# Layer 3's gate silu(x Wz) of a four-layer network: computed in the final stage from x3, where it was computed within layer 1, stored and loaded

## The chip, the cores and the metric

The kernel runs on one core of one Trainium2 chip. The metric is device time in microseconds (us) of one execution. Engines are named as in the profile: PE is TensorE's matmul, PEld its weight load, DVE is VectorE, ACT is ScalarE, POOL is GpSimd, SP is SyncE, which only issues transfers here.

## What is computed

Four layers run one after the other over 4 images of 64 x 64 positions and 128 channels, in float32: a neighbourhood attention (layer 0), a full attention over the 4096 positions of an image (layer 1), a gated mixing with a layer norm (layer 2) and a selective scan in four directions (layer 3). The change concerns layer 3, whose input x is called x3 in the kernel:

```
xz = x @ Win
xb, z = jnp.split(xz, 2, axis=-1)
...                                   # xb: convolution, silu, scans in four directions
y = (y0 + y1 + y2 + y3).transpose(0, 2, 1)
zf = jax.nn.silu(z.reshape(Bb, L, Cd))
yz = y * zf
mu = yz.mean(-1, keepdims=True)
xc = yz - mu
var = (xc * xc).mean(-1, keepdims=True)
yn = gamma * xc / jnp.sqrt(var + 1e-05) + beta
out = yn @ Wout
```

`Win` has 128 rows and 512 columns: 256 for xb and 256 for z, the gate.

## The kernel before

**Tiles and stages.** An image of 4096 positions is cut in 8 chunks of 512 (`CH`). A tile has 128 channels on the partitions and 512 positions beside them; the 256 inner channels of layer 3 are two such tiles, f = 0 and 1. `layers_0_to_2` runs the images one after the other, `layer_3` then all of them together.

**Within an image** layer 1 (`layer_1`) loops over 32 blocks of 128 queries plus two turns. In each turn it computes the scores of one block (L624), the softmax of the one before (maxima turned at L639, spread at L647, subtracted at L650, Exp at L651) and the values of the one before that (L657). At the end of each turn, `between(i)` adds work that has nothing to do with this block: layer 2 of the chunks that are ready (`turn`, `mix`, `add`, `norm`, one after the other for each chunk) and, by `front`, the first part of layer 3. `front` takes chunks of the image before and of this image by a list (`takes`): it loads a chunk of x3 (`load`), projects it to xb (`project`, L799), convolves it over some turns, applies Silu (`activate`), computes the scan's inputs (`lower`) and computes the gate (`gate`, L823 to L832: two products of 128 x 512 at L828, two Silus at L820 and two stores of 256 KB to `zf_d` at L832). In the turns it is called with r == 3, once every four turns. The last chunks of image 3 have no layer 1 beside them; they are written out by turn number in `end`.

**The order.** A scheduler orders each engine's instructions by when they are ready, unless an instruction is tied to the one before it on its engine (`keep_in_program_order`, called `pin`). All PE, DVE, ACT and SP instructions of the final stage are pinned; those on POOL aren't. Transfers issued by SP form one queue in order.

**Layer 3.** The scans (L1207 to L1321) run over pairs of images and directions, and add their outputs in `y_d` and `ys`. The **final stage** is the second block of `layer_3`. It loops over 32 chunks j, with these steps:
- `load` (four chunks ahead): two loads of the scans' sum (`yl`, L1356) and two of the gate (`zc`, L1357), 256 KB each; `load_turned` brings 2 MB an image.
- `add_turned` (two ahead): adds the turned directions on POOL (L1374). For every fourth chunk half of it is copied on ACT (L1371) and added by PE later.
- `times_gate` (one ahead): the product with the gate on DVE (L1379), or for every fourth chunk a sum through PE (L1383) and two products (L1384, L1385).
- `project(j, p)` for each half p: turns (L1398) and projects (L1402) on PE, variances by DVE (L1406, L1407) and by ACT (L1409, L1411).
- `root` (L1419): Sqrt of the variances on ACT; a reciprocal on DVE follows in `give_out` (L1425).
- `give_out` (one behind): scales and adds the bias on DVE (L1429), stores from ACT's queue (L1434).

In a turn j these stand as `load(j+4)`, `project(j, 0)`, `give_out(j-1, 0)`, `add_turned(j+2)`, `times_gate(j+1)`, `project(j, 1)`, `root(j)`, `give_out(j-1, 1)`.

Of the kernel before, what the change touches and what calls it, by code (L numbers as in the profile page):

```python
# [80 lines left out]
@with_exitstack  # L81
def conv_seq(ctx, tc, x, mata, matb, cols, rows, rpb, dtw, convw, sel, out):
    nc = tc.nc
    xf = x.rearrange("b h w c -> b (h w) c")
    of = out.rearrange("b h w c -> b (h w) c")

    dram = ctx.enter_context(tc.tile_pool(name="dram", bufs=1, space=DRAM))
    const = ctx.enter_context(tc.tile_pool(name="const", bufs=1))
    x3_d = [dram.tile([P, L], F32, name=f"x3_d{b}") for b in range(B)]

    def stored(name):
        return [[dram.tile([P, L], F32, name=f"{name}{b}_{f}") for f in range(2)] for b in range(B)]

    ub_d, zf_d = stored("ub_d"), stored("zf_d")
# [11 lines left out]
    fronts = x3_d, ub_d, zf_d, y_d, dbl_d, ct_d, gw_d, bw_d  # L108
# [26 lines left out]
    layer_3(tc, of, dt, na, ident, cl, big, early, *fronts)  # L135


@with_exitstack
def layers_0_to_2(
    ctx, tc, xf, mata, matb, rows, rpb, convw, sel, ident, cl, dram, big, ring, early, x3_d, ub_d, zf_d, y_d, dbl_d, ct_d, gw_d, bw_d  # L140
):
    nc = tc.nc
    wp = ctx.enter_context(tc.tile_pool(name="wa", bufs=1))
# [79 lines left out]
            dma(dst, src)  # L223


    win = wp.tile([P, 2 * DI], F32, name="win")
    nc.sync.dma_start(win, matb[:, MB["win"][0]:MB["win"][1]])
# [467 lines left out]
    def layer_2(b, xt):  # L695
# [47 lines left out]
        def norm(n):  # L743
            mv, rd = kept.pop(n)
            for k in range(4):
                x = xt[:, 4 * n + k, :]
                nc.vector.tensor_scalar(x, x, mv[:, k, 0:1], rd[:, k:k + 1], ALU.subtract, ALU.mult)
            stays = b == B - 1 and n >= 4
            if stays:
                x3 = fresh[n] = tmp.tile([P, CH], F32, name="x3k", tag="g1")  # L750
            else:
                x3 = tmp.tile([P, CH], F32, name="x3", tag="c512", bufs=9)
            transpose_tiles(
                xt, 4 * n, x3,
                lambda o, i: nc.vector.tensor_scalar(
                    in_blocks(o), by_block(i, "r b c"), cl("ln_s"), cl("ln_b"), ALU.mult, ALU.add
                ),
            )
            if not stays:
                nc.sync.dma_start(x3_d[b][:, bass.ts(n, CH)], x3)  # L760

        return turn, mix, add, norm

# [9 lines left out]
    def front(b):  # L773
# [21 lines left out]
        def project(i, n):  # L795
            me = n & 1
            for f in range(2):
                pi = ps_s([P, CH], "pi")
                nc.tensor.matmul(pi, lhsT=win[:, P * f:P * f + P], rhs=x_of[i, n], start=True, stop=True)  # L799
                nc.scalar.copy(xh[:, me, f, 1:RC + 1, :], by_image_rows(pi))  # L800
            row = nc.vector if at_end(i, n) and n > 5 else nc.gpsimd
            if n == 4 and i < b:
                nc.gpsimd.tensor_copy(xh[:, me, :, 0, :], kept_row)
            elif n > 0:
                row.tensor_copy(xh[:, me, :, 0, :], xh[:, 1 - me, :, RC, :])
                row.tensor_copy(xh[:, 1 - me, :, RC + 1, :], xh[:, me, :, 1, :])
# [12 lines left out]
        def silu(i, n, to, of):  # L819
            ins = nc.scalar.activation(to, of, AF.Silu)  # L820
            if not at_end(i, n):
                tc.keep_in_program_order(ins)

        def gate(i, n):
            x = x_of.pop((i, n))
            for f in range(2):
                pz = ps_s([P, CH], "pz")
                nc.tensor.matmul(pz, lhsT=win[:, DI + P * f:DI + P * f + P], rhs=x, start=True, stop=True)  # L828
                zf = tmp.tile([P, CH], F32, name="zf", tag="c512", bufs=9)

                silu(i, n, zf, pz)
                nc.sync.dma_start(zf_d[i][f][:, bass.ts(n, CH)], zf)  # L832

        def tap(n, f, dy, dx):
            r0, r1, c0, c1 = region(n, dy, dx)
# [186 lines left out]
        def end(i):  # L1022

            c = B - 1
            if i in (30, 34, 38):
                n = i // 4 - 2
                load(c, n)
                project(c, n)
            if i == 31:
                gate(c, 5)  # L1030
            if i in (30, 31):
                convolve(c, 4, range(2), i - 30)
            if i == 34:
# [7 lines left out]
                activate(c, 5, True)  # L1041
            if i == 37:
                lower(c, 5)
                gate(c, 6)
            if i == 38:
                convolve(c, 7, (1,), 0)
                convolve(c, 7, (1,), 1)
                for f in range(2):
                    convolve_by_pe(c, 6, f, 1)
                activate(c, 6, True)  # L1050
                convolve_by_pe(c, 7, 0)
                lower(c, 6)
                gate(c, 7)
            if i == 39:
                activate(c, 7, True)
            if i == 40:
# [13 lines left out]
        def turn(i):  # L1070
# [8 lines left out]
            if j < 8:  # L1079
# [7 lines left out]
                elif now and r < 2:  # L1087
                    convolve(*now, range(2), r)
                if r == 3:
                    for c in takes[j]:  # L1090
                        gate(*c)
                    for c in takes[j + 1] if j < 7 else []:
                        load(*c)

# [63 lines left out]


@with_exitstack  # L1160
def layer_3(ctx, tc, of, dt, na, ident, cl, big, early, x3_d, ub_d, zf_d, y_d, dbl_d, ct_d, gw_d, bw_d):
    nc = tc.nc
    def pool(name, bufs=1, **kw):

# [2 lines left out]
    wp = ctx.enter_context(pool("wb"))  # L1167
    gw = wp.tile([P, 2, C], F32, name="gw")
    bw = wp.tile([P, C], F32, name="bw")
    eps = wp.tile([P, 1], F32, name="eps")  # L1170
    ct = wp.tile([W, 2, W], F32, name="ct")

    def place(name, tag, bufs=1):
# [5 lines left out]
    nc.vector.memset(eps, 1e-5)  # L1179
# [38 lines left out]
    with pool("s", 2) as sp, pool("psC", 2, space=PSUM) as psp:  # L1218
# [88 lines left out]
        for j, ((loads, pair), after) in enumerate(zip(todo, todo[1:] + [None])):  # L1307
# [9 lines left out]
            if j == 0:  # L1317
                nc.sync.dma_start(gw, gw_d)
                nc.sync.dma_start(bw, bw_d)
                nc.sync.dma_start(ct[:, 0, :], by_rows(bc_d[B - 1][1])[0])  # L1320
            if j == 18:  # L1321
                turn_c(B - 1, psp.tile([P, 2, CH], F32, name="pt3", tag="dt0", bufs=1)[0:W, 0, 0:W])
# [7 lines left out]
    with pool("o", 2) as op, pool("psD", 2, space=PSUM) as psp:  # L1330
# [18 lines left out]
        def load(j):  # L1349
            b, n = chunks[j]  # L1350
            c = held[j] = Chunk()
            c.yl = op.tile([P, 2, CH], F32, name="yl", tag="yl", bufs=4)
            c.zc = op.tile([P, 2, CH], F32, name="zc", tag="zc", bufs=4)
            lo = L - CH * (n + 1) if b & 1 else CH * n
            for f in range(2):
                pin(nc.sync.dma_start(c.yl[:, f, :], y_d[0][b][f][lo // SC][:, lo % SC:lo % SC + CH]))  # L1356
                pin(nc.sync.dma_start(c.zc[:, f, :], zf_d[b][f][:, bass.ts(n, CH)]))  # L1357

        def add_turned(j):

# [5 lines left out]
            for f, yt in enumerate((yts[b], ys[b])):  # L1366
# [6 lines left out]
                else:  # L1373
                    nc.gpsimd.tensor_tensor(by_rows(c.yc[:, f, :]), by_rows(yn), yr, ALU.add)  # L1374

        def times_gate(j):
            c = held[j]
            if c.sum is None:
                pin(nc.vector.tensor_tensor(c.yc, c.yc, c.zc, ALU.mult))  # L1379
            else:  # L1380
                ps = psp.tile([P, CH], F32, name="ysum", tag="s", bufs=1)
                for i, part in enumerate(c.sum):
                    pin(nc.tensor.matmul(ps, lhsT=ident, rhs=part, start=(i == 0), stop=(i == 1)))  # L1383
                pin(nc.vector.tensor_tensor(c.yc[:, 0, :], ps, c.zc[:, 0, :], ALU.mult))  # L1384
# [2 lines left out]
        def project(j, p):  # L1387
# [3 lines left out]
                c.po = []  # L1391
                c.var = op.tile([P, 4, 2], F32, name="var3", tag="var3", bufs=3)
            py = psp.tile([P, 2, DI], F32, name="py", tag="y", bufs=3)
            po = psp.tile([P, 2, C + 1], F32, name="po3", tag="o", bufs=4)
            for q in range(2):
                ts = bass.ts(2 * p + q, P)
                for f in range(2):
# [18 lines left out]
        def root(j):  # L1416
            c = held[j]
            c.rd = op.tile([P, 4], F32, name="rd3", tag="rd3", bufs=3)
            pin(nc.scalar.activation(c.rd, c.var[:, :, 1], AF.Sqrt, bias=eps))  # L1419

        def give_out(j, p):
            b, n = chunks[j]
            c = held[j]
            if p == 0:
                pin(nc.vector.reciprocal(c.rd, c.rd))  # L1425
                c.ot = op.tile([P, 4, C], F32, name="ot", tag="ot", bufs=3)
            for q in range(2):
                k = 2 * p + q
# [10 lines left out]
        for j in range(-2, last + 1):  # L1439
# [10 lines left out]
                add_turned(j + 2)  # L1450
            if 0 <= j + 1 < last:
                times_gate(j + 1)
            if 0 <= j < last:
                project(j, 1)
                root(j)
# [82 lines left out]
```

## Time and profile before

| | us |
|---|---|
| three runs: median (lowest, highest) | 3702.48 (3697.66, 3703.27) |
| the profiled execution: first to last instruction (span) | 3697.0 |
| layer 1 of image 0 begins (first L639) | 227.5 |
| last product of the layer-1 loops (L657) | 3006.3 |
| scans: first product (L1248) | 3059.4 |
| final stage: first load issued (L1356) | 3527.2 |

The page comes from one execution. The profile gives no time for it but its span, which lies 5.5 us below the median of the runs.

How to read it: a line of the timeline has its start, its time and the number of instructions that run into one another; two products of 128 x 512 in float32 show as four records. A line by stretch has, for each engine, the busy time and the number of instructions, then the granted clock of PE (1.00 is full), the share that the DMA engines were busy, and what they moved. In the 40-slice rows each digit is the busy share of a slice of 92.4 us in tenths.

### The profile page before, as it was taken

How to read it: one execution, taken by the hardware profiler on the slowest of the kernel's cores; microseconds unless marked ns; L12 is line 12 of the kernel's file. 1: busy time of each engine (PE TensorE's matmuls, PEld its weight loads, DVE VectorE, ACT ScalarE, POOL GpSimd, SP SyncE). 2: the span in 40 equal slices, each digit the busy share in tenths (PEclk: the TensorE clock that was granted, in tenths of full speed). 3: DMA queues.
4: the chain of work that ended last, by engine and by line, in shares of the span. 5: the costliest groups of instructions: out<-in, count | busy, mean ns of one | idle time of the engine just before them, and what ended most of it. 6: DMA issues, size and time to landing. Idle time of an engine off the chain costs nothing.

```text
span 3697.0 us, 70138 instructions
## 1 busy us (share of the span) xinstructions
PE 3349.9 (91%) x26774; PEld 2768.1 (75%) x26774; DVE 2796.5 (76%) x5227; ACT 2699.7 (73%) x4387; POOL 1419.4 (38%) x1592
## 2 busy tenths in 40 slices
PE   7999999999999999999999999989999997666647
PEld 4789999966899999667999996779999962222236
DVE  4667788866678878666777886767787767999968
ACT  5856677777677777786777777867777778999934
POOL 6500012244122122451222223512221338999866
PEclk8999999999999999999999999999999995555579
DMA  4200000121010012410121212100100269999998
GB/s 132 64 3 30 13 13 30 60 90 34 18 50 27 33 45 79 134 39 15 42 72 33 76 48 94 45 1 24 47 27 33 70 179 240 217 232 211 209 276 281
DMA packets 188308, 310.95 MB, mean 84 GB/s; under 512 B 22303, under 2 KB 110908, under 8 KB 183068
## 3 DMA queue, kind: packets, MB, share of 16 engines
q1 hardware_dynamic: 145316, 220.27, 17.7%
q0 software_dynamic: 24384, 76.95, 11.7%
q10 hardware_dynamic: 18272, 9.24, 0.9%
q8 instruction: 211, 3.46, 0.4%
q14 instruction: 125, 1.02, 0.1%
HBM read 167.69 MB, written 155.56 MB: 87 GB/s over the span
## 4 chain that ended last, share of the span: by engine, by line
PE 59%; issue 13%; DVE 10%; POOL 8%; ACT 7%; DMA 3%; SPq 1%; DVEq 0%; POOLq 0%; ACTq 0%
PE sc L624 17%; PE po L657 17%; PE pt L502 4%; POOL inp L1259 3%; PE sc L467 3%; PE po L513 2%; POOL y L1301 2%; DVE mx L630 2%; DVE acc L878 1%; PE pp L523 1%; PE pz L828 1%; DVE h L1286 1%; PE pb L647 1%; PE pq L595 1%; PE pk L598 1%
## 5 line engine op out<-in xcount | busy, mean ns | idle before, releaser
L624 PE MATMUL sc<-qT,kT 128*128 128x128 f32 x8192 | 1083.9, 276 | 15.8 <-DVE mx L630 15.8
L657 PE MATMUL po<-v,st 128*128 128x129 f32 x8192 | 1080.6, 275 | 2.0 <-ACT st L651 2.0
L624 PEld LDWEIGHTS sc<-qT,kT 128*128 128x128 f32 x8192 | 1000.9, 193 | 38.8 <-issue 26.6
L657 PEld LDWEIGHTS po<-v,st 128*128 128x128 f32 x8192 | 997.9, 192 | 4.7 <-ACT st L651 2.2
L627 ACT COPY st<-sc 128x512 f32<-128x512 f32 x1024 | 574.8, 584 | 426.2 <-PE sc L624 425.5
L630 DVE TENSOR_TENSOR mx<-mx,sc 128x512 f32<-128x512 f32 x768 | 524.0, 682 | 202.3 <-ACT st L627 178.6
L650 DVE TENSOR_TENSOR st<-st,pb 128x2048 f32<-128x2048 f32 x256 | 574.5, 2280 | 4.9 <-PE pb L647 3.8
L651 ACT ACTIVATE st<-st 128x2048 f32<-128x2048 f32 x256 | 483.2, 1908 | 64.7 <-DVE st L650 64.0
L1248 PE MATMUL pdt<-dbl,dt 8*128 8x512 f32 x512 | 307.3, 1079 | 142.1 <-ACT de L1255 141.1
L1259 POOL TENSOR_TENSOR inp<-de,ub 128x1024 f32<-128x1024 f32 x128 | 409.6, 4393 | 9.0 <-DMA y<-du 4.9
L1248 PEld LDWEIGHTS pdt<-dbl,dt 8*128 8x128 f32 x512 | 114.0, 311 | 332.5 <-ACT de L1255 269.5
L493 POOL TENSOR_SCALAR pr<-pr,sm 128x308 f32<-128x308 f32 (+3 forms) x512 | 243.7, 495 | 219.4 <-DVE sm L491 187.3
L723 POOL TENSOR_TENSOR x<-x,row 128x512 f32<-128x512 f32 x32 | 40.8, 1275 | 692.7 <-PE pt L283 692.7
L869 POOL TENSOR_TENSOR gsum<-gsum,tp 128x504 f32<-128x504 f32 (+1 forms) x177 | 240.7, 1363 | 170.9 <-ACT tp L861 84.1
L485 ACT ACTIVATE pr<-pr,mx 128x308 f32<-128x308 f32 (+3 forms) x512 | 262.6, 517 | 0.0
L1286 DVE TENSOR_TENSOR_SCAN h<-h,end,inp 128x1024 f32<-128x1024 f32 x96 | 221.1, 2346 | 18.3 <-ACT h L1272 8.0
L471 DVE CUSTOM_DVE_ANT_0 pr<-sc,bias_m 128x266 f32<-128x266 f32 (+1 forms) x384 | 152.1, 452 | 103.6 <-PE sc L467 103.6
L502 PE MATMUL pt<-ident,pr 128*88 128x128 f32 (+5 forms) x1472 | 203.8, 275 | 8.1 <-ACT prT L504 7.8
L1301 POOL DMA_DIRECT2D y<-yo x112 | 200.7, 2710 | 10.8 <-DVE yo L1300 7.9
L878 DVE SCALAR_TENSOR_TENSOR acc<-xh,cc,acc 128x512 f32<-128x512 f32 (+3 forms) x250 | 199.3, 818 | 4.6 <-ACT acc L842 3.6
L502 PEld LDWEIGHTS pt<-ident,pr 128*88 128x88 f32 (+5 forms) x1472 | 163.5, 138 | 45.6 <-ACT prT L504 31.6
L504 ACT COPY prT<-pt 110x512 f32<-110x512 f32 (+3 forms) x240 | 139.1, 580 | 65.6 <-PE pt L502 65.6
(234 smaller groups left out, 5170.9 us busy)
## 6 DMA issues: line engine op xcount, KB each, us to landing
y<-yo POOLq DMA_DIRECT2D x112, 512.0 KB, 10.6
y<-y SPq DMA_DIRECT2D x48, 512.0 KB
zf_d<-zf SPq DMA_DIRECT2D x64, 256.0 KB
ub_d<-u SPq DMA_DIRECT2D x64, 256.0 KB
ub<-ub_d SPq DMA_DIRECT2D x16, 1024.0 KB
yl<-y SPq DMA_DIRECT2D x64, 256.0 KB
zc<-zf_d SPq DMA_DIRECT2D x64, 256.0 KB
v_d<-vt SPq DMA_DIRECT2D x32, 256.0 KB
```

The costliest lines, as they stand in the source:

```text
L485: pin(nc.scalar.activation(k.pr[:, h], k.pr[:, h], AF.Exp, bias=k.mx[:, h:h + 1], accum_out=k.sm[:, h:h + 1]))
L502: pin(nc.tensor.transpose(pt[0:n, h, :], k.pr[:, h, at:at + n], ident))
L624: nc.tensor.matmul(ps[:, r, :], lhsT=kT[:, bass.ts(G * g + r, P)], rhs=qT[:, bass.ts(i, P)], start=True, stop=True)
L627: nc.scalar.copy(k.st[:, G * g:G * g + G, :], ps)
L630: nc.vector.tensor_tensor(k.mx, k.st[:, 0:G, :] if g == 1 else k.mx, ps, ALU.max)
L650: nc.vector.tensor_tensor(part, part, pb.unsqueeze(1).to_broadcast([P, 16, P]), ALU.add)
L651: nc.scalar.activation(part, part, AF.Exp)
L657: nc.tensor.matmul(k.po, lhsT=k.st[:, j, :], rhs=v[:, j, :], start=(j == 0), stop=(j == NT - 1))
L1248: nc.tensor.matmul(pdt[j][:, g, :], lhsT=dt[o:o + RANK, P * f:P * f + P], rhs=at(dbl[o:o + RANK, :], k & 2, g0, g0 + CH), start=True, stop ...
L1259: nc.gpsimd.tensor_tensor(by_rows(inp), by_rows(de), at(ub_s[f], b ^ (k & 1), SC * n, SC * n + SC), ALU.mult)
L1286: nc.vector.tensor_tensor_scan(h[:, way], h[:, way], inp[:, way], prev, ALU.mult, ALU.add)
L1301: nc.gpsimd.dma_start(here if f == 1 and k == 3 else there, yo, accum_op=ALU.add)
```

## The change

The gate leaves `front`, and `zf_d` with its stores and loads goes. All chunks of x3 are stored now, those too that stayed on the chip before (chunks 4 to 7 of image 3). The second half of `Win` is loaded as `wz` during the scans. In the final stage a chunk's x3 is loaded (256 KB instead of two loads of 256 KB), and `gates(j + 2)` computes the gate just ahead of `project(j, 1)`. Three more edits come with it: the root is taken on POOL, by an addition of eps and a power of -0.5, in place of ACT's Sqrt and DVE's reciprocal; the PSUM tag "s" gets two buffers, which the gate and the sum share; and the tag "o" of the output sums gets 3 for 4.

```diff
@@ layers_0_to_2: norm, project, gate, turn
-            if not stays:
-                nc.sync.dma_start(x3_d[b][:, bass.ts(n, CH)], x3)
+            nc.sync.dma_start(x3_d[b][:, bass.ts(n, CH)], x3)
...
+            x_of.pop((i, n))
...
-        def gate(i, n):
-            x = x_of.pop((i, n))
-            for f in range(2):
-                pz = ps_s([P, CH], "pz")
-                nc.tensor.matmul(pz, lhsT=win[:, DI + P * f:DI + P * f + P], rhs=x, start=True, stop=True)
-                zf = tmp.tile([P, CH], F32, name="zf", tag="c512", bufs=9)
-
-                silu(i, n, zf, pz)
-                nc.sync.dma_start(zf_d[i][f][:, bass.ts(n, CH)], zf)
...
-                    for c in takes[j]:
-                        gate(*c)
@@ layer_3
-    eps = wp.tile([P, 1], F32, name="eps")
+    wz = wp.tile([P, DI], F32, name="wz")
+    root4 = wp.tile([P, 4], F32, name="root4")
...
+                nc.sync.dma_start(wz, matb[:, MB["win"][0] + DI:MB["win"][1]])
...
-            c.zc = op.tile([P, 2, CH], F32, name="zc", tag="zc", bufs=4)
+            c.xz = op.tile([P, CH], F32, name="xz", tag="xz", bufs=4)
...
-                pin(nc.sync.dma_start(c.zc[:, f, :], zf_d[b][f][:, bass.ts(n, CH)]))
+            pin(nc.sync.dma_start(c.xz, x3_d[b][:, bass.ts(n, CH)]))
...
+        def gates(j):
+            c = held[j]
+            c.zc = op.tile([P, 2, CH], F32, name="zc", tag="zc", bufs=2)
+            for f in range(2):
+                ps = psp.tile([P, CH], F32, name="zs", tag="s", bufs=2)
+                pin(nc.tensor.matmul(ps, lhsT=wz[:, bass.ts(f, P)], rhs=c.xz, start=True, stop=True))
+                pin(nc.scalar.activation(c.zc[:, f, :], ps, AF.Silu))
...
-                ps = psp.tile([P, CH], F32, name="ysum", tag="s", bufs=1)
+                ps = psp.tile([P, CH], F32, name="ysum", tag="s", bufs=2)
...
-            po = psp.tile([P, 2, C + 1], F32, name="po3", tag="o", bufs=4)
+            po = psp.tile([P, 2, C + 1], F32, name="po3", tag="o", bufs=3)
...
-            pin(nc.scalar.activation(c.rd, c.var[:, :, 1], AF.Sqrt, bias=eps))
+            nc.gpsimd.tensor_scalar(c.rd, c.var[:, :, 1], 1e-5, 1.0, ALU.add, ALU.mult)
+            nc.gpsimd.tensor_tensor(c.rd, c.rd, root4, ALU.pow)
...
-                pin(nc.vector.reciprocal(c.rd, c.rd))
...
             if 0 <= j + 1 < last:
                 times_gate(j + 1)
+            if j + 2 < last:
+                gates(j + 2)
             if 0 <= j < last:
                 project(j, 1)
                 root(j)
```

The three calls of `gate` in `end` (chunks 5, 6 and 7 of image 3) go too, and `win` is loaded with 256 columns for 512.

More of the change, by code (lines that the diff above doesn't have):

```diff
@@ L92, in stored @@
         return [[dram.tile([P, L], F32, name=f"{name}{b}_{f}") for f in range(2)] for b in range(B)]
-    ub_d, zf_d = stored("ub_d"), stored("zf_d")
+    ub_d = stored("ub_d")
     dbl_d = [dram.tile([NDBL, L], F32, name=f"dbl_d{b}") for b in range(B)]
@@ L107, in conv_seq @@
     ]
-    fronts = x3_d, ub_d, zf_d, y_d, dbl_d, ct_d, gw_d, bw_d
+    fronts = x3_d, ub_d, y_d, dbl_d, ct_d, gw_d, bw_d
     ident = const.tile([P, P], F32, name="ident")
@@ L134, in conv_seq @@
     layers_0_to_2(tc, xf, mata, matb, rows, rpb, convw, sel, ident, cl, dram, big, ring, early, *fronts)
-    layer_3(tc, of, dt, na, ident, cl, big, early, *fronts)
+    layer_3(tc, of, matb, dt, na, ident, cl, big, early, *fronts)
 @with_exitstack
 def layers_0_to_2(
-    ctx, tc, xf, mata, matb, rows, rpb, convw, sel, ident, cl, dram, big, ring, early, x3_d, ub_d, zf_d, y_d, dbl_d, ct_d, gw_d, bw_d
+    ctx, tc, xf, mata, matb, rows, rpb, convw, sel, ident, cl, dram, big, ring, early, x3_d, ub_d, y_d, dbl_d, ct_d, gw_d, bw_d
 ):
@@ L223, in layers_0_to_2 @@
             dma(dst, src)
-    win = wp.tile([P, 2 * DI], F32, name="win")
-    nc.sync.dma_start(win, matb[:, MB["win"][0]:MB["win"][1]])
+    win = wp.tile([P, DI], F32, name="win")
+    nc.sync.dma_start(win, matb[:, MB["win"][0]:MB["win"][0] + DI])
     wx = wp.tile([P, 2, HD], F32, name="wx")
@@ L1028, in end @@
                 project(c, n)
-            if i == 31:
-                gate(c, 5)
             if i in (30, 31):
@@ L1043, in end @@
                 lower(c, 5)
-                gate(c, 6)
             if i == 38:
@@ L1052, in end @@
                 lower(c, 6)
-                gate(c, 7)
             if i == 39:
@@ L1160, in layer_3 @@
 @with_exitstack
-def layer_3(ctx, tc, of, dt, na, ident, cl, big, early, x3_d, ub_d, zf_d, y_d, dbl_d, ct_d, gw_d, bw_d):
+def layer_3(ctx, tc, of, matb, dt, na, ident, cl, big, early, x3_d, ub_d, y_d, dbl_d, ct_d, gw_d, bw_d):
     nc = tc.nc
@@ L1178, in layer_3 @@
     ys = [place("y0", "kT")] + [place(f"y{b}", "ring", 5) for b in range(1, B)]
-    nc.vector.memset(eps, 1e-5)
+    nc.vector.memset(root4, -0.5)
     bc_d = [[dbl_d[b][RANK:RANK + 1, :], dbl_d[b][RANK + 1:RANK + 2, :], ct_d[b]] for b in range(B)]
```

## The prediction

> **What bounds the kernel now.** I read the page's first two parts first, then single stretches of the timeline, then busy time by stretch. The whole span is 3697.0 us. The three runs shown are 3697.66, 3702.48 and 3703.27, that is 0.7 to 6.3 us above that span, the median 5.5. All sums below are made against the span, and 5.5 is added at the end.
>
> The page says that TensorE (PE) is nearly always busy until the scans:
>
> ```profile
> PE 3349.9 (91%) x26774; PEld 2768.1 (75%) x26774; DVE 2796.5 (76%) x5227; ACT 2699.7 (73%) x4387; POOL 1419.4 (38%) x1592
> PE   7999999999999999999999999989999997666647
> PEclk8999999999999999999999999999999995555579
> ```
>
> A busy PE need not be a limit, so I look at two turns of layer 1's loop in image 0. A turn runs from one transposed maximum (L639) to the next. This is the PE timeline of a turn with layer 2's `mix` (L708, L712, L716) and no gate:
>
> ```profile
> 376.53 0.27 PE L639 MATMUL pt<-ident,mx 128*128 128x128 f32 x1
> ...
> 387.58 0.29 PE L708 MATMUL pr<-rs,ma 128*128 128x8 f32 x2
> 387.72 1.10 PE L712 MATMUL pg<-x2T,ma 128*128 128x512 f32 x2
> 388.67 1.02 PE L716 MATMUL pl<-x2T,w_le 128*128 128x512 f32 x2
> 389.52 1.05 PE L624 MATMUL sc<-qT,kT 128*128 128x128 f32 x8
> ...
> 393.10 0.27 PE L639 MATMUL pt<-ident,mx 128*128 128x128 f32 x1
> ```
>
> And of a turn with `mix` and the gate (L828):
>
> ```profile
> 440.72 0.27 PE L639 MATMUL pt<-ident,mx 128*128 128x128 f32 x1
> ...
> 453.71 1.88 PE L828 MATMUL pz<-xc,win 128*128 128x512 f32 x4
> 455.43 1.05 PE L624 MATMUL sc<-qT,kT 128*128 128x128 f32 x8
> ...
> 459.00 0.27 PE L639 MATMUL pt<-ident,mx 128*128 128x128 f32 x1
> ```
>
> The first turn takes 16.57 us, the second 18.28. The difference, 1.71, is what the gate's four records hold PE (453.71 to 455.43, 1.72). PE works without a gap, so here its work is time.
>
> The final stage is another matter. Busy time by stretch (PE, PEld, DVE, ACT, POOL, granted clock, DMA share, GB/s):
>
> ```profile
> 3637.00:3667.00 30.00, 23.60 (x180) 20.44 (x179) 27.00 (x76) 14.92 (x55) 23.77 (x14) 1.00 1.00 335
> 3547.30:3687.00 139.70, 105.91 (x774) 92.32 (x775) 115.88 (x310) 61.97 (x222) 93.09 (x54) 0.94 0.90 305
> ```
>
> and its chain of waits, one period of four chunks apart:
>
> ```profile
> 3651.31 0.68 DVE yc L1385
> ...
> 3667.63 0.68 DVE yc L1385
> ```
>
> A period is 16.32 us, 4.08 a chunk, with VectorE (DVE) busy 27.0 of 30. From the first gate product (3547.3) to the last (3686.9) are 31 chunks, 126.5 us at that pace, and 139.6 were taken; 13.1 went to late loads (POOL's add waits 8.48 us for `yl` at 3589.9).
>
> **What goes from layer 1.** 30 of 32 chunks have their gate in or at the end of the layer-1 loops (120 records of L828 up to 3006), the last two behind them.
> - 28 chunks inside full turns: 28 x 1.72 = 48.2. Later turns with a gate take 18.6 to 18.7, not 18.28, with the 0.3 to 0.4 around ScalarE (ACT) work; if that goes as well, 21 turns return up to 7 more. Three turns of 20.0 us (image 1's runs from 1120.9 to 1140.9) have PE idle 1.5 for DVE, and PE waits 2.0 in the turn behind; there the gate may be free, 5 less. I take 3 less: 45.
> - Two chunks at 2986.6, in the last turn: 3.4. Their second pair of Silus, with two table loads, sits between the halves of the last Exp (1.28 + 1.08 + 1.28 = 3.64 on ACT from 2997.08); PE waits 2.00 there. 2.0 more.
> - Chunk 6 of image 3: four records on the chain at 3035.8, 1.7.
> - Chunk 7: ACT does two Silus until 3056.3 ahead of the u of the same chunk (L912), whose sum is ready at 3051.8; ACT is free at 3052.8. I count 2.7 of these 3.4.
>
> Sum 54.8, say 55, with 47 to 66 as ends. The 64 stores (L832) leave SP's queue, where they wait 679.6 us in all; DMA is at a share of 0.15 there, so I count nothing. Four added x3 stores take the place of eight gate stores in the tail: nothing. The table loads mostly stay, since the u of another chunk follows the gate in the same turn. The scans (3059 to 3530) lose nothing and only start earlier; the one added load of 128 KB vanishes among their transfers.
>
> **What comes to the final stage.** For each chunk two products of 128x512 (1.72 of PE), two Silus (2 x 0.597 on ACT), two small GpSimd (POOL) operations; a 0.298 Sqrt on ACT and a 0.145 reciprocal on DVE go. Loads fall from four of 256 KB to three: 49.2 MB in the last 172 us become 40.8, which at 335 GB/s is 122 us. That is under any time below, so the 13.1 of late loads go, and the next late thing is PE.
>
> PE's pace per chunk, from its starts at 3656.33, 3656.79, 3657.69: turns 0.46, projection 0.90, both twice: 2.72. With gates 4.44. Every fourth chunk has the sum through PE (3665.10 to 3666.82, 1.72): 6.16. Four chunks 19.5, against 16.32. 29 chunks at 4.87 and the last two, without gates, at 4.08 make 149.4: +9.8 is the floor.
>
> On top stands a loop, because the po buffers fall from 4 to 3. po(j+2,0) now needs the output sums of j's second half, and these follow the root. From the start of po(j,0): 0.90, gates 1.72, turn 0.46, po 0.90, is 3.98; 0.2 to ACT; its bias, Square and accumulator read, 1.0; the root P on POOL, 0.1; then on DVE two sums 0.52, the gate product 1.66, statistics 0.55, two sums 0.52, and 0.1 back. That is 8.6 + P for two chunks. Of P the trace shows no row: a power on POOL isn't in it. Below stand the 0.10 memset of 128x1, above the 4.39 product of 128x1024. Nearest is the tensor_scalar of 128x128 (0.372), so two operations on 4 columns get 0.5. The loop then gives 4.55 a chunk, 6.27 with the sum: 152.6, **+13**.
>
> Behind the root on POOL stand the adds of chunk j+3; ahead, if the order differs. The POOL lines are not pinned, and the trace shows that POOL takes what is ready: L723 runs behind PE's transposes (692.7 us of idle end there) ahead of L719, which the code writes first. An add becomes ready when po(j,1) has read its buffer, 0.9 ahead of the root. With one add of 1.6 ahead the loop is 9.7, 4.85 a chunk: 161.3, **+22**. With both, 5.65: 184, +45. I take +18, between the first two. The start (POOL waits for a `y` accumulate until 3544.3) and the end (the power instead of Sqrt and reciprocal) change by under 1.
>
> ACT has 0.34 + 1.33 + 0.27 + 0.38 (output issue) + 1.2 = 3.5 a chunk, under the pace. Square and Copy run at 3553 without a table load, then behind the Sqrt load as well, so they seem to be at home in several tables; with Silu's the trace doesn't show Square. Bounds: nothing, or two loads of 1.28 a chunk, 6.1 on ACT, +46. I take nothing, as both tables seen had them; the other end lies where the late root below does.
>
> The Trainium skill, "ScalarE: Activation LUTs", section "Table sets: the hidden batching unit", says that cheap functions (it names relu, copy, identity, abs) are in every set, Square not among the names; with a switch at its 2.66 us twice a chunk ACT would need 8.8 and my sum would end near 3770.
>
> The product on DVE takes 1.21 alone and up to 2.53, POOL's add 1.50 to 2.53: they hinder each other, and the rows I use hold that. The skill's "SBUF — State Buffer", section "SBUF: two separate sides", calls the port that they share an exclusive lock: a DVE instruction with two SBUF inputs shuts a reading POOL instruction out for its whole length. By that the small root could wait for a product, some 1.4 in the loop, 20 us in all, and my sum would end near 3685.
>
> **Sum.** -55 + 18 = -37: span 3660, median 3665.
>
> **Rivals.**
> - *Root behind both adds* (0.16): +45, so -10, 3692. For it: POOL's readiness order. Against: the second add starts only after the root is ready.
> - *More comes back* (0.14): 66 in layer 1 and only the floor of 10: -56, 3646. For it: 18.6 against 18.28. Against: DVE is busy 19 to 20 us in the turns behind the gates.
> - *The power is dear* (0.06): one POOL instruction sets the final stage. It decides from P = 3.4, where the loop is 6.0, 6.43 with its share of the sums, and 29 of these eat the 55. At 4.4 it gives 6.93: 209, +70, 3717, slower. Against: only 4 columns.
> - *Little is gained in layer 1* (0.04): DVE or ACT take over as the limit, 25 instead of 55: 3695. Against: gapless PE rows.
> - The forecast, +13 to +22 (0.60).
>
> The range holds the forecast, the better case, the late root and the fourth, with 4 us of turn-to-turn scatter at the lower end: 3642 to 3696; the dear power and the outer parts of the forecast's own bounds stay out. Faster by over 0.2% (7.4 us, about what a measurement here can tell from none): 0.60 + 0.14 + 0.15, and half of the fourth, 0.91. Within: 0.04. Slower: 0.05.
>
> **What would show it.** Turns of the layer-1 loop with `mix` at 16.6 to 17.0; no L828 and Exp halves together at the end. In the final stage PE the busiest, granted clock 1.0, four chunks 19.5 to 22 apart, DMA share about 0.75, no table load but one. Wrong if POOL's root is longer than 1 us, if POOL does adds ahead of it, or if turns stay above 18.

## The result and the profile after

| | kernel before | changed kernel |
|---|---|---|
| median of 4 runs each (lowest, highest), us | 3701.84 (3697.66, 3703.27) | 3755.14 (3749.41, 3756.36) |
| span of the profiled execution | 3697.0 | 3752.2 |

The ratio is 1.0143, with an interval from 1.0128 to 1.0157: the changed kernel takes 1.4% longer. The prediction was 3665, in a range that ended at 3696. The spans divide like this (layer-1 loops: first L639 to the last product of values; tail: from there to the scans' first product; scans: to the final stage's first load; final stage: to the end):

| us | before | after | difference |
|---|---|---|---|
| layer-1 loops | 2779.1 | 2758.8 | -20.3 |
| tail | 52.8 | 58.4 | +5.6 |
| scans | 467.8 | 471.7 | +3.9 |
| final stage | 169.8 | 236.4 | +66.6 |
| within it, first to last gate product (31 chunks) | 139.5 | 204.4 | +64.9 |

What was ahead of the loops is 0.6 shorter; together that is the 55.2 between the spans. Below, "the stage's 31 chunks" is always the last row.

The page's 40 slices of the changed kernel, PE and the granted clock:

```profile
PE   7999999999999999999999999999999976666587
...
PEclk9999999999999999999999999999999965555699
```

The picture is that of before up to the scans. A turn with `mix` (PE, from one L639 to the next, with layer 2's product between) is now

```profile
1252.97 0.33 PE L639 MATMUL pt<-ident,mx 128*128 128x128 f32 x1 [0.91 <-DVE mx L635]
...
1269.35 0.27 PE L639 MATMUL pt<-ident,mx 128*128 128x128 f32 x1
```

16.38 us, and no L828 is left. That turn in the kernel before took 18.57. The saving is there; other turns gave it back, as the first experiment below shows. The final stage by stretch, with the columns of the prediction's view:

```profile
3625.00:3655.00 30.00, 24.57 (x129) 15.89 (x127) 13.81 (x39) 12.64 (x37) 18.52 (x19) 1.00 0.49 158
3535.20:3739.70 204.50, 167.38 (x892) 113.13 (x890) 102.16 (x280) 88.06 (x253) 115.87 (x113) 0.98 0.51 170
```

The clock is full and the DMA share has fallen from 0.90 to 0.51, as forecast. But no engine is full: PE 24.6 of 30, POOL 18.5, DVE 13.8 where it had 27.0. A stage that is slow with no engine full points to a loop of waits. Its longest wait (engine and line, what it waits for, total, times, longest):

```profile
DVE ot L1423 <- POOL rd L1414: 80.3, 29, 3.4
```

POOL's own timeline in one turn shows why (start, time, line, operation, and in brackets the idle time before it and what ended it). With it stand the last of ACT's sums of squares that the root needs, the instruction of DVE that waits, and two second halves of the projection on PE, po(j,1) and po(j+1,1), with po(j+1,0) and the gates of chunk j+3 between them:

```profile
3638.51 1.53 POOL L1360 TENSOR_TENSOR yc<-yl,cb 128x512 f32<-128x512 f32 x1 [2.00 <-PE po L1396]
3640.00 1.53 POOL L1360 TENSOR_TENSOR yc<-yl,y 128x512 f32<-128x512 f32 x1
3641.61 0.19 POOL L1413 TENSOR_SCALAR rd<-var 128x4 f32<-128x4 f32 x1
3641.89 1.02 POOL L1414 TENSOR_TENSOR rd<-rd,root 128x4 f32<-128x4 f32 x1
```

```profile
3639.09 0.19 ACT L1405 ACTIVATION_READ_ACCUMULATOR sq<-py,nm 128x1 f32 x1
```

```profile
3642.94 0.61 DVE L1423 SCALAR_TENSOR_TENSOR ot<-po,rd,bw 128x128 f32<-128x128 f32 x2 [3.04 <-POOL rd L1414]
```

```profile
3637.30 1.13 PE L1396 MATMUL po<-gm,yc 128*128 128x129 f32 x8 [1.53 <-DVE ot L1423]
...
3643.69 1.13 PE L1396 MATMUL po<-gm,yc 128*128 128x129 f32 x8 [0.92 <-DVE ot L1423]
```

When the products of po(j,1) have read their tile (PE 3637.30 to 3638.43), both adds of chunk j+3 may write it, and both run ahead of the root of chunk j. That root has all it needs at 3639.28, ahead of the second add (3640.00), and the add runs first all the same, in every turn that has two; so POOL's order isn't that of readiness; the scheduler had set it. The root takes 0.19 and 1.02, DVE's sums of the first half 0.61, and they release the buffer that the next po(j+1,1) needs; PE starts it at 3643.69. From 3637.30 to 3643.69 is 6.39 us: one chunk. While DVE stands at `ot`, all that is behind it on DVE (the gate product, the statistics, the sums) waits too, and PE behind these.

### The profile page after: what moved, and what is told of

Its sections match the earlier page's. It is cut to its first block, busy times and chain, and to the rows that moved or that the text cites. A ratio compares the mean times of both kernels' runs of the same rounds, so it can differ in the third digit from the quotient of the medians.

```text
span 3752.2 us, 69998 instructions
## 1 busy us (share of the span) xinstructions
PE 3371.9 (90%) x26774; PEld 2775.7 (74%) x26774; DVE 2790.2 (74%) x5195; ACT 2697.0 (72%) x4363; POOL 1437.6 (38%) x1656
## 3 DMA queue, kind: packets, MB, share of 16 engines
q1 hardware_dynamic: 132212, 196.15, 15.7%
## 4 chain that ended last, share of the span: by engine, by line
PE 54%; DVE 13%; ACT 10%; issue 10%; POOL 9%; DMA 3%; SPq 0%; POOLq 0%; ACTq 0%; DVEq 0%
PE sc L624 15%; PE po L657 15%; PE pt L502 4%; POOL inp L1244 3%; DVE mx L630 3%; PE sc L467 2%; PE po L513 2%; POOL y L1286 2%; ACT st L651 2%; DVE acc L868 2%; ACT st L627 2%; DVE st L650 2%; PE pp L523 1%; POOL yc L1360 1%; PE pi L798 1%
## 5 line engine op out<-in xcount | busy, mean ns | idle before, releaser
L624 PE MATMUL sc<-qT,kT 128*128 128x128 f32 x8192 | 1088.3, 277 | 14.8 <-DVE mx L630 14.7
L650 DVE TENSOR_TENSOR st<-st,pb 128x2048 f32<-128x2048 f32 x256 | 574.8, 2280 | 18.9 <-PE pb L647 18.5
L859 POOL TENSOR_TENSOR gsum<-gsum,tp 128x504 f32<-128x504 f32 (+1 forms) x177 | 232.2, 1318 | 139.1 <-ACT gsum L847 70.7
L1271 DVE TENSOR_TENSOR_SCAN h<-h,end,inp 128x1024 f32<-128x1024 f32 x96 | 221.0, 2346 | 20.3 <-ACT h L1257 10.0
L868 DVE SCALAR_TENSOR_TENSOR acc<-xh,cc,acc 128x512 f32<-128x512 f32 (+3 forms) x250 | 226.1, 913 | 6.4 <-ACT acc L832 5.1
L719 POOL TENSOR_TENSOR o<-o,rt 128x512 f32<-128x512 f32 x32 | 34.1, 1067 | 402.7 <-DVE o L718 397.0
```

What stands on the lines that cost most here:

```text
L624: nc.tensor.matmul(ps[:, r, :], lhsT=kT[:, bass.ts(G * g + r, P)], rhs=qT[:, bass.ts(i, P)], start=True, stop=True)
L650: nc.vector.tensor_tensor(part, part, pb.unsqueeze(1).to_broadcast([P, 16, P]), ALU.add)
L868: nc.vector.scalar_tensor_tensor(acc, x, c, acc, ALU.mult, ALU.add)
```

## Layer 1 and the tail: two losses beside the saving

**u's Silu.** Before, `gate` stood at the end of its turn, and `activate`, the Silu of another chunk's u, came just behind. ACT before, one such turn:

```profile
1273.42 1.28 ACT L820 ACT_TABLE_LOAD   x1
1274.71 1.22 ACT L820 ACTIVATE zf<-pz 128x512 f32<-128x512 f32 x2
1275.83 1.05 ACT L820 ACTIVATE u<-acc 128x1024 f32<-128x1024 f32 x1
```

One load served both, right behind layer 2's Sigmoid. After, with the gate's Silus gone, the Silu of the same chunk's u is placed two turns earlier by the scheduler, behind the softmax and away from the Sigmoid, with a load of its own and a reload for Exp behind it:

```profile
1232.08 1.28 ACT L820 ACT_TABLE_LOAD   x1
1233.38 1.06 ACT L820 ACTIVATE u<-acc 128x1024 f32<-128x1024 f32 x1
...
1241.10 1.28 ACT L651 ACT_TABLE_LOAD   x1
```

Four turns in a row, the first of them with `mix`, took 18.62, 18.54, 15.88 and 15.07 before (from 1192.0, with the gate in the first), and 16.76, 18.15, 16.21 and 17.81 after (from 1184.0, with this u at the end of the third and the reload in the fourth): the gate's turn won 1.9, and the turn with the reload lost 2.7.

*e4_silu_first.* In `between`, u's Silu is moved to the head of its turn, ahead of the convolution:

```diff
+            for c, at in zip(whole, u_at):
+                if c and i == at and at < 32:
+                    activate(*c, False)
             now = whole[j] if j < 8 else None
...
-                if c and i == at:
-                    activate(*c, at >= 32)
+                if c and i == at and at >= 32:
+                    activate(*c, True)
```

> The changed kernel with the Silu of the convolved chunk (u) issued at the head of its turn's extra work, right behind the Sigmoid of layer 2, where the gate's Silus carried it before; the final stage is as in the changed kernel. Theory (the u Silu lost its place beside the gate's and pays a table load and a load back to Exp in a turn of its own, where PE waits 1 to 2.6 us): layer 1's loops, first transposed maximum to last value product, take 2725 to 2742 us where the changed kernel has 2758.8 and the one before 2779.1. Rival (with the gate gone DVE or ACT set the pace of the turns): 2752 to 2762.

Measured (one run): 3719.49. Loops 2725.8, 33.0 less than after and 53.3 less than before; table loads up to the end of the loops 158, against 177 and 169; the four turns 16.92, 18.55, 15.07, 15.10. The final stage is unchanged (204.5). So the gate's removal was worth about what the prediction counted in the loops (50.4 of its 55), and 33.0 of it was lost to the place of u's Silu.

**The ring of tiles.** In the tail, ACT of the changed kernel stands still here:

```profile
3014.35 1.33 ACT L950 ACTIVATE du<-u,col 128x512 f32<-128x512 f32 x2 [8.68 <-DMA y<-du]
```

`du` takes its tile from the tag `c512`, a ring of 9. With the gate's two `zf` gone, fewer tiles pass between two `du`, and the tile whose turn it is was one whose accumulating store (issued by POOL at 3001.82) hadn't landed. SP had started copies of 512 KB from 2998.88 on; that the store stood behind them is argued from these times, not shown.

*c11_more_buffers.* As e4_silu_first, with `bufs=11` for 9 wherever the tag `c512` stands.

> u's Silu at the head of its turn, and 11 buffers for the tag c512 in place of 9; the whole computation. Theory for the tail (with the gate's two tiles gone from this ring, the ninth tile back of a du is a du whose store stands behind copies of the scans' sums, and ACT waits 8.7 us for it): the stretch from the last layer-1 product to the scans' first product falls from 58.2 to 50-54 us, the layer-1 loops stay at 2724-2730, the whole 3711-3716. Rival (the copies and stores are late whatever the ring): 57-59, the whole 3717-3722.

Measured (one run): 3707.85; the wait is gone (`du` starts at 2969.17 right behind the Silu), the tail is 51.1 for 58.2, loops 2722.6. The theory holds for the tail; loops and whole came out a little below what was expected. With both edits loops and tail are 58.2 us below those of before; the prediction had 54.8.

## The final stage: which part costs, and through what

*e5_root_alone.* The kernel before with the root part alone; the gate stays in layer 1:

```diff
-            po = psp.tile([P, 2, C + 1], F32, name="po3", tag="o", bufs=4)
+            po = psp.tile([P, 2, C + 1], F32, name="po3", tag="o", bufs=3)
...
-            pin(nc.scalar.activation(c.rd, c.var[:, :, 1], AF.Sqrt, bias=eps))
+            nc.gpsimd.tensor_scalar(c.rd, c.var[:, :, 1], 1e-5, 1.0, ALU.add, ALU.mult)
+            nc.gpsimd.tensor_tensor(c.rd, c.rd, root4, ALU.pow)
...
-                pin(nc.vector.reciprocal(c.rd, c.rd))
```

with 2 buffers for `ysum`.

> The kernel before with one part of the change: root on POOL by addition and power, 3 buffers for the output sums, 2 for the sum through PE; the gate stays in layer 1 and is loaded. Theory (loop of one turn through POOL): the gate's products aren't in the loop, so the final stage is nearly as slow as with the whole change, 185 to 204 us from the first to the last gate product where the kernel before has 139.5, span 3740 to 3760. Rival (the products and Silus of the gate slow the final stage): 139 to 155.

Measured (one run): 3750.18; the stage's 31 chunks 184.7, 45 more than before.

*e7_no_gate_product.* The other way round: the changed kernel with `pin(nc.scalar.copy(c.zc[:, f, :], c.xz))` for product and Silu, which leaves the gate out.

> The changed kernel without the two gate products on PE and their Silus in the final stage: two ACT copies of the loaded x3 stand in zc instead, and the root stays on POOL. This leaves the gate out, so only its time counts. Theory (the root is most of the loss, the gates about 20 us): the stage from the first to the last gate product falls from 204.4 to 178-190 us, as where the root alone was moved (184.7). Rival (the gates are the price): 140-155.

Measured (one run): 3731.54; 184.9. The two agree: the root is 45 of the 65, the gate's work 20. As ACT copies for as long as it took for a Silu (0.62 and 0.60 us), these 20 are the price of the products on PE and of the waits that they bring.

*e6_no_power.* `ALU.mult` for `ALU.pow`, which leaves the power out.

> The changed kernel with the power on POOL replaced by a multiplication with the same constant, in the same place; this leaves the power out, so only its time counts. A multiplication of 4 columns should take about what the addition takes, 0.2 us, for 1.02. Theory (the root's whole length stands in the loop that DVE closes): about 0.8 us a chunk less over 31 chunks, so from the first to the last gate product 177-187 us for 204.4, the whole 3728-3738. Rival (only its place behind two adds counts, POOL would wait for data in any case): 197-205, the whole above 3745.

Measured (one run): 3729.63; 183.3, 21.1 less. The group of the multiplication (mean in ns behind the comma):

```profile
L1414 POOL TENSOR_TENSOR rd<-rd,root 128x4 f32<-128x4 f32 x26 | 5.2, 201 | 2.2
```

0.82 us shorter per chunk gave 0.68 per chunk: the power's length stands in the loop nearly whole, so the loop closes in each chunk. A loop of two chunks would have given 0.41.

*e1_root_first.* The adds and the root's two instructions are pinned on POOL in the order of the code, so that the root comes ahead of the adds of chunk j+3.

> The changed kernel, with the POOL instructions of the final stage tied to the order of the code, so that the root of chunk j runs ahead of the two adds of chunk j+3 and not behind them. Theory (a loop of one turn): the second projection of a turn needs the output-sum buffer that the first output sums of the chunk before give back; these wait for the root, and the root stands behind two adds of 1.52 us, which wait for the projection before. Without the adds in it the loop is about 4.0 us and PE sets the pace, so the 31 chunks from the first to the last gate product take 152 to 162 us where they took 204.4, and the span is near 3705. Rival (the power's own 1.21 us, or the gate's products on PE with their waits, set the pace): 190 to 204, span above 3738.

Measured (one run): 3722.69; 177.8, 26.6 less, between the theory's range and the rival's. Of the rest, DVE still waits 31.4 us for the root in 29 waits, and two groups have become longer:

```profile
L1360 POOL TENSOR_TENSOR yc<-yl,y 128x512 f32<-128x512 f32 x29 | 58.5, 2019 | 0.0
...
L1373 DVE TENSOR_TENSOR yc<-yc,zc 128x1024 f32<-128x1024 f32 x22 | 44.3, 2012 | 0.0
```

In the changed kernel these means were 1.52 and 1.21: there DVE waited while POOL worked. Now they meet, as here:

```profile
3621.34 1.54 POOL L1360 TENSOR_TENSOR yc<-yl,cb 128x512 f32<-128x512 f32 x1
3622.83 2.50 POOL L1360 TENSOR_TENSOR yc<-yl,y 128x512 f32<-128x512 f32 x1
```

```profile
3621.92 2.03 DVE L1373 TENSOR_TENSOR yc<-yc,zc 128x1024 f32<-128x1024 f32 x1
```

The add that was running keeps its 1.54; the product that starts beside it takes 2.03, and the next add 2.50. How much of the 177.8 comes from this, no run isolates.

*e2_po4.* `bufs=4` for `po3` and, to make room, `bufs=2` for `py`.

> The changed kernel with 4 buffers for the output sums again, and 2 for the turned tiles, where it has 3 and 3; POOL's order as it is, root behind the adds. Theory (the loop is closed by the third buffer): with four, a projection waits for output sums of half a turn earlier, the loop spans more than one turn, and the 31 chunks take 160 to 175 us for 204.4. Rival (the root's lateness alone is enough, whatever the buffers, or the gate's products are the price): 195 or more.

Measured (one run): 3751.38; 200.0. My theory named the third buffer as what closes the loop, and that failed: one more buffer gave 4 us, though with one `py` less beside it, so the two are not apart. DVE still waits for the root (56.7 us in 25 waits), and as its instructions are pinned in order, product and statistics wait behind it. That this closes the loop whatever the buffers is argued, not shown by a run of its own.

*e3b_root_off_pool.* No root on POOL; in the place of the old reciprocal DVE adds 1e-5 in one instruction, and the power is left out:

```diff
-            nc.gpsimd.tensor_scalar(c.rd, c.var[:, :, 1], 1e-5, 1.0, ALU.add, ALU.mult)
-            nc.gpsimd.tensor_tensor(c.rd, c.rd, root4, ALU.pow)
...
+                pin(nc.vector.tensor_scalar(c.rd, c.var[:, :, 1], 1e-5, 1.0, ALU.add, ALU.mult))
```

> The changed kernel with the two POOL instructions of the root taken out. In the place of the old reciprocal, at the head of give_out, DVE adds 1e-5 to the variances in one instruction on 4 columns. This leaves out the power (the output is scaled by the variance itself), so only its time counts. Theory (the root on POOL, 1.2 us behind two adds, holds DVE's sums, and DVE in order holds the products and PE): the time from the first to the last gate product falls from 204.4 to 150-170 us, and the whole from 3755 to 3700-3720. Rival (two more products and two Silus a chunk are the price, through PE, ACT and the shared buffers): it stays above 185, the whole above 3735.

Measured (one run): 3714.23; 161.6. By stretch PE is the bound now:

```profile
3590.00:3620.00 30.00, 29.66 (x165) 20.23 (x164) 23.92 (x60) 15.88 (x48) 16.20 (x11) 1.00 0.61 189
```

This is the state that the prediction had drawn, PE the busiest, but not at its price: 161.6 is 22.1 more than before, where its floor had 9.8.

## Another place for the root

If POOL is the wrong engine, is there a right one? In all kernels here u's Silu stands first in its turn, as in e4_silu_first, and all of them do the whole computation. The ratios are against the kernel before.

*abs_root_u_first.* `pin(nc.scalar.activation(c.rd, c.var[:, :, 1], AF.Abs_reciprocal_sqrt, bias=eps))` in the root's place.

> The whole computation. u's Silu at the head of its turn, and the root as one ACT instruction in Sqrt's old place (absolute value's reciprocal square root, pinned), with no reciprocal. It tells what the root costs on ACT. If its table holds Silu, Square and Copy too, the final stage has no reload: gate products over 150-160 us, the whole 3663-3678. If not, there are two loads of 1.28 us a chunk (62 in all), ACT needs about 6.1 a chunk and DVE waits for it: 185-210, the whole 3702-3728. The theory names no table; I expect the second.

Measured: 3688.69, ratio 0.9955 (0.9938 to 0.9972); 180.1. The loads are there, two a chunk (the stretch is 150 us, 26 chunks):

```profile
L1416 ACT ACT_TABLE_LOAD x25 | 32.1, 1283 | 0.4
...
L1371 ACT ACT_TABLE_LOAD x24 | 30.8, 1283 | 0.4
```

and ACT is busy 27.9 to 28.6 of 30 until 3660. I had expected 185 to 210 and 3702 or more; it came out faster. A chunk takes 5.8, with ACT as the bound, where the changed kernel took 6.6 in its loop: even with two loads a chunk, ACT is a better place than the queue on POOL. The switch that the prediction quoted at 2.66 costs half of that here: a load takes 1.283, and the next activation starts 0.02 behind its end at most, so ACT doesn't need the 8.8 a chunk that would follow from 2.66. *abs_root_ring* adds the 11 buffers:

> The whole computation. As abs_root_u_first, with 11 buffers for c512. Theory (the tail's 7 us is independent of the final stage): 3678-3686 for 3688.7, 0.4 to 0.7% below the kernel before. Rival (the final stage's start shifts and eats it): within 3 us of 3688.7.

Measured: 3678.13, 0.9933 (0.9916 to 0.9949), as expected.

*newton_u_first.* The root on DVE at the head of `give_out`, by a first value from the bits and two Newton steps:

```diff
+                pin(V.tensor_scalar(x, c.var[:, :, 1], 1e-5, 1.0, ALU.add, ALU.mult))
+                pin(V.tensor_single_scalar(w.bitcast(i32), x.bitcast(i32), 1, op=ALU.logical_shift_right))
+                pin(V.tensor_scalar(c.rd.bitcast(i32), w.bitcast(i32), -1.0, float(0x5f3759df), ALU.mult, ALU.add))
+                for _ in range(2):
+                    pin(V.tensor_tensor(w, c.rd, c.rd, ALU.mult))
+                    pin(V.scalar_tensor_tensor(w, w, -0.5, x, ALU.mult, ALU.mult))
+                    pin(V.scalar_tensor_tensor(c.rd, w, 1.5, c.rd, ALU.add, ALU.mult))
```

> The whole computation. Two edits of the changed kernel: u's Silu at the head of its turn, behind layer 2's Sigmoid (worth 33 us when alone), and the root computed on DVE at the head of give_out, by one addition, two instructions on the bits for a first value, and two Newton steps of three instructions, all on 4 columns. Theory: no engine waits for POOL's root any more; DVE gains nine instructions of 0.07 to 0.15 us in place of a wait, so it becomes about equal to PE: gate products over 155-172 us, the whole 3670-3692. Rival (small dependent instructions cost DVE 0.2 us or more each, 1.8 a chunk): 180 or more, 3697 or more, no faster than before.

Measured: 3715.91, 1.0039 (1.0025 to 1.0053); 203.1. The theory failed. The shift took 1.127 us in the mean, the six behind it 0.162 each, and DVE was busy 27 of 30. I took the shift for a slow instruction:

*newton_no_shift.* Without the shift; the first value is `x.bitcast(i32)` times -0.5 plus the constant.

> The whole computation. As newton_u_first, without the shift, which took 1.127 us: the first value comes from one multiplication by -0.5 and an addition on the bits read as an integer (0.17 us). DVE per chunk then has 1.36 for four sums, 1.22 for two statistics, 1.22 for the product and 1.50 for the root, 5.3 for 6.4. Theory (DVE was the bound there, 27 of 30 us busy): gate products over 165-175 us for 203, the whole 3676-3692. Rival (PE and DVE wait for one another in turn, so less comes back): 185-195, 3696-3708.

Measured: 3708.09, 1.0015 (1.0003 to 1.0026); 198.7. Failed again, and now the instruction that follows the first addition takes 1.161 where it had taken 0.170. The timeline tells why:

```profile
3557.17 1.52 POOL L1361 TENSOR_TENSOR yc<-yl,y 128x512 f32<-128x512 f32 x1
3557.27 1.44 DVE L1425 TENSOR_SCALAR rd<-vx 128x4 int32<-128x4 int32 x1
...
3563.48 0.17 DVE L1425 TENSOR_SCALAR rd<-vx 128x4 int32<-128x4 int32 x1
```

It ends with POOL's second add, 0.03 behind it, and in turns with only one add it takes 0.17. Of the 32 such instructions of the stage, 22 meet an add, and each of these ends 0.02 to 0.03 behind that add. It is a wait that the profile books as work.

*newton_act_stats.* As newton_no_shift with 11 buffers for `c512`, and both variances of a half by ACT's Square: DVE less loaded, the wait left in.

> The whole computation. As newton_no_shift, with 11 buffers for c512, and the variance of both blocks of a half by ACT's Square (0.474 and 0.193 for the accumulator) where DVE took one by its statistics (0.61): DVE 4.1 a chunk, ACT about 4.8, PE 4.87 by the prediction's floor. Theory: PE becomes the bound, gate products over 155-166 us, the whole 3658-3678. Rival (ACT, in order with the Silus, is late for both): 172 or more, 3683 or more.

Measured: 3703.64, 1.0000 (0.999 to 1.001); 199.6, with DVE at 22 of 30 and PE at 24 to 25. DVE's load was not the bound: failed, and it points to the wait. ACT, the rival, is busy under 19 of 30.

*newton_psum.* As newton_no_shift with 11 buffers, and two of the root's small tiles in unused columns of the buffer of `po`, in PSUM:

```diff
+                x, w = c.po[1][:, 0, C + 1:C + 5], c.po[1][:, 1, C + 1:C + 5]
```

so that no small instruction has all operands in SBUF.

> The whole computation. As newton_no_shift with 11 buffers for c512, and two of the root's four small tiles in unused columns of the output sums' PSUM buffer, so that no small DVE instruction has all its operands in SBUF. Theory (DVE's small instruction waited for POOL's add, through the memory port that they share, and held the lock against nothing of its own length): the first value takes about 0.2 us for 1.16, the first addition about 0.2 for 0.41; gate products over 168-182 us for 199, the whole 3675-3692. Rival (the instruction itself is long, from the integers or from waiting for the result before it): it stays above 0.8 us, 195-200, the whole 3698-3706.

Measured: 3669.15, 0.9909 (0.9894 to 0.9924); 167.7. The first value and the first addition (mean in ns behind the comma):

```profile
L1424 DVE TENSOR_SCALAR rd<-po 128x4 int32<-128x4 int32 x24 | 3.9, 162 | 0.8
L1423 DVE TENSOR_SCALAR po<-var 128x4 f32<-128x4 f32 x24 | 3.6, 152 | 0.0
```

0.162 for 1.161, 0.152 for 0.413. Of the 32 first values 29 meet an add of POOL here, and none takes longer than 0.17. So the wait went with the place of the operands, and the instruction as such isn't long.

The Trainium skill, "SBUF — State Buffer", section "SBUF: two separate sides", says that a DVE instruction in a two-port mode, or with two SBUF inputs against a reading POOL instruction, and a POOL instruction exclude each other for a whole instruction, and "VectorE: DVE Perf Modes", section "Why PSUM operands drop a tier", that an operand in PSUM keeps DVE out of the two-port mode. The 1.44 beside a running add, the 0.17 without one and the 0.162 from PSUM agree with both; the port itself, and the mode of an instruction, no view here shows.

*newton_psum_act.* newton_psum with ACT's Square for both variances.

> The whole computation. As newton_psum, and the variances of both blocks of a half by ACT's Square, as in newton_act_stats. DVE about 4.1 a chunk, ACT 4.8, PE 4.87. Theory (the port again, and the loops through DVE end early enough): gate products over 155-170 us, the whole 3660-3680. Rival (the loop of po(j,0), root, DVE's sums and po(j+1,1) sets the pace whatever DVE's load): 185 or more, 3690 or more.

Measured: 3666.46, 0.9905 (0.989 to 0.992); 164.9, and PE is the bound:

```profile
3570.00:3600.00 30.00, 29.84 (x172) 21.22 (x171) 21.11 (x78) 22.07 (x73) 14.63 (x10) 1.00 0.60 186
```

Both newton_psum kernels beat the kernel before and the changed one; their intervals overlap each other.

## Why the prediction was wrong, point by point

The step that failed is the root's way through POOL. The prediction took it at 0.5 us, behind one add at most, in a loop that closes once in two chunks: 4.55 to 4.85 us a chunk. The runs show 1.30 us, behind every add that POOL has, in a loop that closes in each chunk: 6.39 us. With the root off POOL, 42.8 of the stage's added 64.9 us are gone (e3b).

- **The layer-1 products** (48.2 in the turns). Right in size: with u's Silu moved the loops give 53.3, where the prediction had 50.4.
- **"The table loads mostly stay, since the u of another chunk follows the gate in the same turn."** Wrong: without the gate, u's Silu is placed two turns earlier and loads its table by itself. The loops have 8 loads more than before, 19 more than with the Silu moved back, and this place costs 33.0 us.
- **The tail** (1.7 and 2.7). Counted as a gain; it became 5.6 longer, by the ring of tiles. I looked at the DMAs and the queues, and not at which buffers the removed tiles had spaced.
- **The floor of PE in the final stage** (4.44 a chunk, 6.16 with the sum, 19.5 for four). Too low: where PE is the bound (newton_psum_act, `zs` at 3563.27, 3568.36, 3573.14, 3579.64 and 3584.22), four chunks take 20.95, that is 0.37 more a chunk. In the chunk from 3568.36, 0.34 more come from the two `po`, with 1.13 and 0.96 for 0.90 each, and from a turn, with 0.52 for 0.46. Why they are longer stays open.
- **The root's price P, taken as 0.5.** Measured 0.19 + 1.02 and the gap between, 1.30 from 3641.61 to 3642.91. The bounds held it, the choice by the nearest row didn't. The wait of the small root for a product, priced at 20, doesn't show: the power took 1.01 to 1.05 in all 32 chunks, while DVE stood waiting for it.
- **The loop, "po(j+2,0) now needs the output sums of j's second half", 8.6 + P for two chunks.** Too long a way round. With three buffers po(j+1,1) already needs the sums of j's *first* half, and these wait for the root of both halves: the loop closes in one chunk, as the timeline and e6 show. The buffer isn't all of it: with four, e2 still took 200.0, and DVE, in order, still waited for the root.
- **Adds ahead of the root.** Taken as none or one; all that POOL has are ahead, two in three turns of four. The argument against, that the second add starts only after the root is ready, was true (3640.00 against 3639.28) and decided nothing, as the scheduler had set POOL's order. The rival "Root behind both adds" named the mechanism, at 5.65 a chunk and +45; measured were 6.39 in such a turn and +65 in all. Its place was right, its loop, P and the floor too short.
- **Late loads and hidden steps.** Right: late loads went, the share of DMA fell (0.51; I had 0.75, of a shorter stage), Square and Copy ran in Silu's table without a reload, the clock was full.

Together: 55 was 14.7 in loops and tail, 18 was 64.9. Of these 64.9, 42.8 are the root's, and 22.1 stay when PE is the bound, for 9.8. That newton_psum_act, at 3666.46, ends near the predicted 3665 is luck, and no support for it: its loops and tail are 62.0 shorter and its final stage is 28.5 longer, for 55 and 18. The 3.9 in the scans seem to lie in their first 30 us (DVE busy 15.7 there, 19.6 in e4_silu_first, where the scans take 468.2); what makes them stays open.

## What to carry to other kernels

A small instruction that is put on an engine with large, ready work stands behind all of that work: price its place in the queue and the loop that its result closes (which buffer, which half, how many turns on) before its length. When an operation is removed, look at what it did for others: the table that it loaded, the order that it fixed, the buffers that it put between two uses of a ring. Where a tiny instruction shows a long duration, look at what the other engine does until just that end.

## What the runs showed of the hardware

- A power of 128x4 on POOL takes 1.02 us, a multiplication of the same size 0.20.
- A DVE instruction of 128x4 with one input, from SBUF to SBUF, took up to 1.46 us beside a POOL add of 1.52, and 0.17 without it or, add or not, with an operand in PSUM; the wait is recorded as its duration, not as idle time.
- DVE's six instructions with two SBUF inputs took 0.162 each; none of them met an add, so nothing is shown of them.
- ACT's table for Silu serves Square and Copy too (no load among 59 of each between 3540 and 3735 of the changed kernel); the absolute reciprocal root needs another, 1.283 us for each change.
